# Written order for the transfers of one queue, late side stores, and four copies moved from VectorE to ScalarE, in a linear attention and mixture-of-experts kernel

## The chip, the core and the metric

The kernel runs on one core of a Trainium2 chip. A core has five engines with instruction streams of their own: TensorE (matrix products), VectorE, ScalarE (activation functions and copies), GpSimd (called POOL in the profile) and SyncE (SP), which here issues most of the DMA transfers. The metric is the device time of one execution in microseconds; less is better. Three timed executions of the kernel before gave 733.79 us in the median (732.57 to 734.19).

## What is computed

Two sublayers follow each other, each on normalized input and with its output normalized and added back. The first is a linear attention over 8 batches of 512 rows by 256 columns, the second a mixture of 8 experts of which each row uses two. `_layernorm` has no scale or shift.

```python
x = L0_attn_x                                   # (8, 512, 256)
x = x + _layernorm(_L0_attn_ref(_layernorm(x), Wq, bq, Wk, bk, Wv, bv, gamma))
x = x + _layernorm(_L0_ffn_ref(_layernorm(x), W1, b1, W2, b2, gate_W, shared_W, shared_b, gamma, beta))

# inside _L0_ffn_ref, flat has 4096 rows of 256
probs = softmax(flat @ gate_W)
topk_w, topk_idx = top_k(probs, 2)
combine = (one_hot(topk_idx, 8) * (topk_w / topk_w.sum(-1))[..., None]).sum(1)
out = 0.5 * gelu(flat @ shared_W + shared_b)
for e in range(8):
    h = gelu(flat @ W1[e] + b1[e])              # 256 -> 1024
    out = out + combine[:, e:e+1] * (h @ W2[e] + b2[e])
out = layernorm(out) * gamma + beta
```

All data are 32-bit floats.

## The kernel before

**Fronts.** `front(b)` computes, for one batch of 512 rows, the attention sublayer, the shared part of the second sublayer and the routing. It is a generator whose pieces are interleaved with those of other batches by `front_round`, after a table of starting rounds. On the way it stores three things in DRAM: the rows after the first sublayer (`x1_d`, line 542; the profile calls this tensor `x_d`), the shared part, which is where the sums of the second sublayer begin (`acc_d`, line 572), and the eight weights of each row (`comb_d`, line 620). GpSimd then scatters every row twice, once for each chosen expert, into slots of the DRAM tensor `xs` (line 669). A row in `xs` carries its 256 values, its eight weights and its number.

`comb_d`, `x1_d` and `shift_d` are also read by a dense pass at the end of the program (from line 1111), which computes rows by all experts. It runs only if the routing overflowed its slots, and it does not run with this data: `n_steps` is zero.

**Jobs.** A job is a stretch of 256 slots of one expert, or a tile of 128 slots. There are 37 jobs, numbered 0 to 36 here; the list is built at lines 685 to 694. Jobs 29 and 33 to 36 are tiles of 128 whose expert is known only at run time (`MORE = 5`). For each job:

- `fetch(k)` loads the slots, `xr` (line 705); it is called two jobs ahead, at the start of job k - 2.
- `turn(k)` transposes them on TensorE into two PSUM buffers and copies these to `rT`: the first half on VectorE, the second on ScalarE (`transposed`, lines 361 and 362). It is called before the last one or two row tiles of job k - 1.
- `routed(k)` computes the first layer in eight pieces on TensorE (`ph`, line 727, into a pool of four PSUM buffers), the activation on ScalarE (`h`, line 732), then the second layer (`po`, line 765) for every 128 rows. VectorE adds the bias and scales (`y`, lines 769 and 773), and GpSimd adds the rows into `acc_d` by an indirect DMA (line 776). Each such scatter waits for the scatters of the job before it. The last two jobs (`CLOSE = 2`) scatter nothing: their rows are added on TensorE, in `close`.

Weights are loaded by `load_w`: first-layer weights (line 207) go round three buffers, second-layer weights and biases (lines 210 and 212) round two. It is called when a job ends and the next one has another expert.

**Endings.** `back(b)` finishes a batch when all its scatters are in: it loads the sums (`accb`, line 831) and the rows of the first sublayer (`xb`, line 834), `finish_rows` normalizes twice on VectorE with square roots and the last addition on GpSimd (lines 801 to 823), and line 841 stores the output. A hand-written plan ties these steps to pieces of jobs: batches 0 to 4 lie under jobs 16 to 30, batches 5 to 7 under jobs 33 to 36. Batch 7 goes through `close` instead: at line 849 ScalarE adds a shift to `xb`; TensorE gathers in `fin` the sums (line 855) and the rows of the last two jobs (line 864); VectorE normalizes.

**What sets the order.** The streams of TensorE, VectorE and ScalarE keep the order in which the program writes them (the `manual_schedule` at line 969). GpSimd keeps the written order through `in_turn`, which chains each instruction behind the one before with `behind`, an ordering without a wait. SP's transfers had no such chain: a scheduler could put a transfer ahead of others that are written before it. One pair was chained by hand: the first `xr` load after the reading of the expert numbers, through `turns["SP"]`. In every stream an instruction that waits holds up all that stand behind it.

Of the kernel before, what the change touches and what calls it, by code (L numbers as in the profile page):

```python
# [16 lines left out]
def kernel(  # L17
# [21 lines left out]
    nc = tc.nc  # L39
# [54 lines left out]

    turns = {"on": False, "last": None, "dmas": []}

    def behind(ins, name):
        tc.add_manual_dep(  # L100
# [17 lines left out]
        return ins  # L118


    xs = dram.tile([SLOTS, DX], F32, name="xs")


# [11 lines left out]

    def load_x(b):
        t = act.tile([P, NT, D], F32, tag="x", name=f"x_{b}", bufs=XB)
        nc.sync.dma_start(t, x[b].rearrange("(p t) d -> p t d", t=NT))
# [7 lines left out]

    NK = 2 * ND
    wn = const.tile([P, NK, D + 1], F32, name="wn")
    nc.sync.dma_start(wn[:, 0:ND, 0:D], Wk.rearrange("(o p) i -> p o i", p=P))
    nc.sync.dma_start(wn[:, ND:NK, 0:D], Wq.rearrange("(o p) i -> p o i", p=P))  # L150
    rows = E * NH
    NR = rows + 3 * ND
    col_stage = act.tile([NR, P], F32, tag="h", name="col_in", bufs=10)
    nc.sync.dma_start(col_stage[0:rows, :], b1.rearrange("e (c p) -> (e c) p", p=P))
    for j, v in enumerate((bk, bq, bv)):
        r = rows + j * ND
        nc.sync.dma_start(col_stage[r : r + ND, :], v.rearrange("(c p) -> c p", p=P))
    load_x(1)

    NV = D + 2  # L160
    wvx = const.tile([P, ND, NV], F32, name="wvx")
    nc.sync.dma_start(wvx[:, :, 0:D], Wv.rearrange("(c p) i -> p c i", p=P))
    bqb = const.tile([P, D], F32, name="bqb")
    nc.sync.dma_start(bqb, bq.partition_broadcast(P))
    bkb = const.tile([P, D], F32, name="bkb")
    nc.sync.dma_start(bkb, bk.partition_broadcast(P))
    gam = const.tile([P, 1], F32, name="gam")
    nc.sync.dma_start(gam, attn_gamma.partition_broadcast(P))

    wsg = const.tile([P, ND, D + E], F32, name="wsg")  # L170
    nc.sync.dma_start(wsg[:, :, 0:D], shared_W.rearrange("(c p) d -> p c d", p=P))
    nc.sync.dma_start(wsg[:, :, D : D + E], gate_W.rearrange("(c p) e -> p c e", p=P))
    bsh = const.tile([P, D], F32, name="bsh")
    nc.sync.dma_start(bsh, shared_b.partition_broadcast(P))
    load_x(2)

    for b in range(3, XB):
# [2 lines left out]

    pad = const.tile([P, CT, DX], F32, name="pad")
    nc.vector.memset(pad, 0.0)
    nc.sync.dma_start(acc_d[B * C :, :].rearrange("(p t) d -> p t d", p=P), pad[:, :, 0:D])
    nc.gpsimd.iota(
        pad[:, :, DX - 1].bitcast(I32), pattern=[[1, CT]], base=B * C, channel_multiplier=CT
    )
    for e in range(E):
        nc.sync.dma_start(
            xs[e * CAP : (e + 1) * CAP, :].rearrange("(j p t) d -> p j (t d)", p=P, t=CT),
            pad.rearrange("p t d -> p (t d)").unsqueeze(1).to_broadcast([P, CAP // CS, CT * DX]),  # L190
        )
    nc.sync.dma_start(
        xs[E * CAP :, :].rearrange("(j p) d -> p j d", p=P),
        pad[:, 0, :].unsqueeze(1).to_broadcast([P, MORE, DX]),
    )
# [2 lines left out]
    def load_w(e, which=(1, 2), name=""):  # L198

        v = ids[e - E] if e >= E else e  # L200

        def of(w):
            return w[bass.ds(v, 1)] if e >= E else w[v : v + 1]

        if 1 in which:
            w1[e] = act.tile([P, ND, H], F32, tag="w1", name=f"w1_{name}{e}", bufs=NW1)
            nc.sync.dma_start(w1[e], of(W1).rearrange("o (c p) h -> p (o c) h", p=P))
        if 2 in which:
            w2[e] = act.tile([P, NH, D], F32, tag="w2", name=f"w2_{name}{e}", bufs=NW2)
            nc.sync.dma_start(w2[e], of(W2).rearrange("o (c p) d -> p (o c) d", p=P))  # L210
            b2b[e] = act.tile([P, D], F32, tag="b2", name=f"b2_{name}{e}", bufs=NW2)
            nc.sync.dma_start(b2b[e], of(b2).rearrange("o d -> (o d)").partition_broadcast(P))
# [4 lines left out]
    nc.sync.dma_start(fgam, ffn_gamma.partition_broadcast(P))  # L217
    fbet = const.tile([P, D], F32, name="fbet")
    nc.sync.dma_start(fbet, ffn_beta.partition_broadcast(P))

# [135 lines left out]
            pts.append(pt[:, 0 : src.shape[1] * P])  # L356
        return pts

    def transposed(dst, src, name):
        pts = transposes(src, name)  # L360
        nc.vector.tensor_copy(dst[:, 0, :], pts[0])  # L361
        nc.scalar.copy(dst[:, 1, :], pts[1])

    def mid(name):
        return act.tile([P, ND, NV], F32, tag="mid", name=name, bufs=10)

    scatters, fills = [], {}

    shifts = const.tile([P, B, NT], F32, name="shifts")

# [1 line left out]
    def front(b):  # L372
# [169 lines left out]
        nc.sync.dma_start(rows_of(x1_d, b), xt)  # L542
        if b + XB < B:
            load_x(b + XB)
        stats = ln_stats([xt[:, t, :] for t in range(NT)], f"c{b}")
# [23 lines left out]
            )  # L569
        yield "A"  # L570
        nc.scalar.activation(acc, acc, AF.Gelu)
        st = nc.sync.dma_start(rows_of(acc_d, b), acc)
        unordered(st, "acc")
        fills[b] = st.ins

# [40 lines left out]
        ))  # L616
        in_turn(nc.gpsimd.tensor_tensor(row[:, :, D : D + E], wb, both, ALU.add))
        in_turn(nc.gpsimd.tensor_copy(row[:, :, DX - 1].bitcast(I32), token[:, b, :]))

        nc.sync.dma_start(rows_of(comb_d, b), row[:, :, D : D + E])  # L620


        shape3 = [P, NT, E]
# [73 lines left out]
    def fetch(k):  # L697
        if k >= len(jobs):
            return
        e, s0, s1 = jobs[k]  # L700
        nt = (s1 - s0) // P
        assert s0 < FIRST or not fronts
        xrs[k] = act.tile([P, CT, DX], F32, tag="xr", name=f"xr_{k}", bufs=4)[:, 0:nt, :]
        r0 = e * CAP + s0 if e < E else E * CAP + (e - E) * P
        ld = nc.sync.dma_start(xrs[k], xs[r0 : r0 + s1 - s0, :].rearrange("(p t) d -> p t d", t=nt))
        if "SP" in turns:
            behind(ld, turns.pop("SP"))
        unordered(ld, "scatter", [ins for b, ins in scatters if s0 >= FIRST or b <= EARLY])

    def turn(k):  # L710
        if k >= len(jobs):
            return
        e, s0, s1 = jobs[k]
        rTs[k] = act.tile([P, ND, CS], F32, tag="rT", name=f"rT_{k}", bufs=2)[:, :, 0 : s1 - s0]
        transposed(rTs[k], xrs[k][:, :, 0:D], f"r{k}")

    def routed(k):
        e, s0, s1 = jobs[k]
# [109 lines left out]
    def back(b):  # L828
        acc = act.tile([P, NT, D], F32, tag="acc", name=f"accb_{b}", bufs=4)
        last = max(n for (e, s1), n in ends.items() if s1 <= room(b, e))  # L830
        ld = nc.sync.dma_start(acc, rows_of(acc_d, b))
        unordered(ld, "acc", [fills[b], *adds[last - 1]])
        xt = act.tile([P, NT, D], F32, tag="x", name=f"xb_{b}", bufs=XB)
        nc.sync.dma_start(xt, rows_of(x1_d, b))
        yield
        if b < B - 1:
            yield from finish_rows(
                [acc[:, t, :] for t in range(NT)], [xt[:, t, :] for t in range(NT)],
                shifts[:, b, :], f"{b}", True,
            )  # L840
            nc.sync.dma_start(out[b].rearrange("(p t) d -> p t d", t=NT), xt)
        else:
            yield from close(acc, xt)


    def close(acc, xt):
# [47 lines left out]
        for h, (mv, rs) in enumerate(parts):  # L894
            for m, t in enumerate(halves[h]):
                nc.vector.tensor_scalar(
                    acc[:, t, :], acc[:, t, :], mv[:, m, 0:1], rs[:, m : m + 1],
                    ALU.subtract, ALU.mult,
                )
            t0, t1 = halves[h][0], halves[h][-1] + 1  # L900
            nc.vector.tensor_tensor(xt[:, t0:t1, :], xt[:, t0:t1, :], acc[:, t0:t1, :], ALU.add)
            nc.sync.dma_start(
                out[b].rearrange("(p t) d -> p t d", t=NT)[:, t0:t1, :], xt[:, t0:t1, :]
            )

# [11 lines left out]
    def check_room():  # L917
        G = len(groups)
        pcnt = bank("p_cnt")[:, 0, 0 : (G + 2) * E].rearrange("p (s e) -> p s e", e=E)
        for s, b in enumerate([*groups, EARLY, B - 1]):  # L920
# [20 lines left out]
        nc.sync.dma_start(  # L941
            shift_d.rearrange("(b p t) o -> p b (t o)", b=B, p=P), shifts
        )
        shape = [P, MORE, E]
# [263 lines left out]
```

## Time and profile before

The profiled execution took 734.14 us, of which 732.4 us lie between its first and its last instruction (the span). Times in the profile count from the start of the span.

| engine | busy, us | share of the span | instructions |
|---|---|---|---|
| TensorE, products | 677.7 | 93% | 3359 |
| VectorE | 285.0 | 39% | 1096 |
| ScalarE | 233.1 | 32% | 540 |
| GpSimd | 294.1 | 40% | 419 |

The page cuts the span into 40 slices. From 165 us to 696 us TensorE's busy share is 9 (90% or more) in every slice but one, at 220 to 238 us. It is lower in several slices of the fronts and in the last two. The DMA engines moved 142.24 MB, 194 GB/s over the span.

| transfer | count | KB each | median us from issue to landing |
|---|---|---|---|
| `w`, either layer's weights | 70 | 1024 | 6.2 |
| `b`, bias of the second layer | 35 | 128 | 6.5 |
| `xr`, 256 slots | 32 | 265 | 2.9 |
| `xr`, 128 slots | 5 | 132.5 | 2.1 |
| `accb` | 8 | 512 | 4.7 |
| `xb` | 8 | 512 | 4.1 |
| `comb_d` store | 8 | 16 | 2.8 |
| scatter into `acc_d` | 67 | | 5.2 |

How to read the lines shown further on. A line of a timeline has the start and the length in us, the engine, the line of the program, the operation, what is written and read, the shape and the count; in brackets the engine's idle time before it and what ended that. A line of the view of waits has who waited for whom, then the total in us, the number of times and the longest. A line of the view of stretches has the stretch, its length, the busy time of TensorE's products, of its weight loads, of VectorE, ScalarE and GpSimd, then the granted clock of TensorE (1.00 is full), the busy share of the DMA engines and GB/s. SPq is SP's queue, which issues transfers; `x1`, `x2` are counts. The chain of waits goes back from the last instruction, at each step to what released it.

### The profile page before, as it was taken

To read this page: it belongs to the slowest core of one execution; us is meant where nothing else is said; L and a number is where in the kernel's file an instruction comes from. 1 tells how busy PE (TensorE), PEld (TensorE's weight loads), DVE (VectorE), ACT (ScalarE), POOL (GpSimd) and SP (SyncE) were. 2 spreads that over 40 slices of the span, in tenths; PEclk is the share of its full clock that TensorE was granted. 3 is DMA by queue.
4 is the path that set the end of the run, shared out by engine and by line. 5 is a ranking of instruction groups with operands and counts; after the bars stand their busy time and mean duration, and the time that the engine had idled before them with its cause. 6 is when DMAs were issued, how large, how long until landed. Compare 5 with 4: busy or idle time off the path is not lost.

```text
span 732.4 us, 10181 instructions
## 1 busy us (share of the span) xinstructions
PE 677.7 (93%) x3359; PEld 591.3 (81%) x3359; DVE 285.0 (39%) x1096; ACT 233.1 (32%) x540; POOL 294.1 (40%) x419
## 2 busy tenths in 40 slices
PE   6998997939998999999999999999999999999981
PEld 4887786727887888888888888888888888988860
DVE  3658868854545143111111112314132132511555
ACT  4444534314331423223223322322332232322430
POOL 3304318775564625122122113433625235442392
PEclk9999999978998999999999999999999999999996
DMA  7994123443377868667667667556686886977841
GB/s 236 381 354 156 72 74 145 148 160 136 112 216 197 252 184 225 200 187 217 174 205 191 190 201 210 156 129 186 205 234 182 259 257 166 287 221 202 267 134 60
DMA packets 88855, 142.24 MB, mean 194 GB/s; under 512 B 11158, under 2 KB 63324, under 8 KB 88796
## 3 DMA queue, kind: packets, MB, share of 16 engines
q1 hardware_dynamic: 76076, 124.05, 52.2%
q0 software_dynamic: 12720, 17.47, 12.1%
q8 instruction: 29, 0.48, 0.3%
q14 instruction: 30, 0.25, 0.1%
HBM read 101.68 MB, written 39.82 MB: 193 GB/s over the span
## 4 chain that ended last, share of the span: by engine, by line
PE 82%; DVE 10%; POOL 2%; DMA 2%; issue 2%; ACT 1%; SPq 0%; POOLq 0%; DVEq 0%
PE ph L727 32%; PE po L765 31%; PE pg L402 3%; PE psh L561 3%; PE py L526 2%; PE pa L482 2%; PE pt_r L353 2%; PE pq L468 1%; PE pt_x L353 1%; DVE x L539 1%; PE puq L424 1%; PE puk L424 1%; DVE junk L440 1%; DVE st_c L332 1%; DMA acc_d<-y,xr 1%
## 5 line engine op out<-in xcount | busy, mean ns | idle before, releaser
L727 PE MATMUL ph<-rT,w 128*128 128x256 f32 (+1 forms) x1184 | 248.7, 368 | 3.6 <-DVE rT L361 3.6
L765 PE MATMUL po<-w,h 128*128 128x256 f32 x1104 | 244.7, 379 | 0.0
L727 PEld LDWEIGHTS ph<-rT,w 128*128 128x128 f32 x1184 | 214.7, 192 | 31.6 <-DVE rT L361 4.4
L765 PEld LDWEIGHTS po<-w,h 128*128 128x128 f32 x1104 | 207.0, 190 | 26.5
L776 POOL DMA_INDIRECT acc_d<-y,xr x67 | 105.4, 1573 | 291.6 <-DVE y L773 268.8
L732 ACT ACTIVATE h<-ph,cols 128x256 f32<-128x256 f32 x256 | 120.9, 473 | 310.8 <-PE ph L727 310.6
L769 DVE TENSOR_TENSOR y<-po,b 128x256 f32<-128x256 f32 x69 | 29.2, 424 | 180.3 <-PE po L765 180.3
L361 DVE COPY rT<-pt_r 128x256 f32<-128x256 f32 (+1 forms) x37 | 15.0, 404 | 170.4 <-PE pt_r L353 166.8
L669 POOL DMA_INDIRECT xs<-xn,slot x64 | 64.7, 1011 | 21.2 <-issue 17.5
L526 PE MATMUL py<-wm,xT 128*128 128x256 f32 x128 | 29.2, 380 | 3.8 <-DVE wm L517 3.8
L561 PE MATMUL psh<-wsg,xfT 128*128 128x264 f32 x128 | 30.0, 388 | 1.5 <-DVE xfT L361 1.5
L526 PEld LDWEIGHTS py<-wm,xT 128*128 128x128 f32 x128 | 23.7, 189 | 7.9 <-DVE wm L517 3.7
L561 PEld LDWEIGHTS psh<-wsg,xfT 128*128 128x128 f32 x128 | 24.1, 191 | 5.7 <-DVE xfT L361 1.9
L482 PE MATMUL pa<-wk,g 128*128 128x258 f32 x64 | 17.2, 415 | 9.9 <-DVE acc L566 9.9
L732 ACT ACTIVATE h<-ph,b1m 128x128 f32<-128x128 f32 x40 | 14.6, 367 | 30.2 <-PE ph L727 27.0
L402 PE MATMUL pg<-xn 128*128 128x128 f32 (+1 forms) x128 | 23.9, 341 | 0.0
L773 DVE TENSOR_SCALAR y<-y,xr 128x256 f32<-128x256 f32 x64 | 22.7, 355 | 2.3
L353 PE MATMUL pt_r<-identd,xr 128*128 128x128 f32 x138 | 21.5, 274 | 1.8 <-DMA xr<-xs 1.2
L482 PEld LDWEIGHTS pa<-wk,g 128*128 128x128 f32 x64 | 13.0, 207 | 12.4 <-DVE acc L566 10.3
L402 PEld LDWEIGHTS pg<-xn 128*128 128x128 f32 x128 | 21.1, 201 | 2.3 <-DVE xn L530 0.2
L445 POOL TENSOR_TENSOR inv<-sq,mhalf 128x4 f32<-128x4 f32 x8 | 8.5, 1059 | 32.5 <-DVE sq L440 32.4
L353 PEld LDWEIGHTS pt_r<-identd,xr 128*128 128x128 f32 x138 | 17.2, 143 | 5.2 <-ACT h L732 1.4
(195 smaller groups left out, 645.7 us busy)
## 6 DMA issues: line engine op xcount, KB each, us to landing
w<-in_L_ffn_W_dram SPq DMA_DIRECT2D x70, 1024.0 KB, 6.2
xs<-pad SPq DMA_DIRECT2D x8, 1060.0 KB, 15.2
xr<-xs SPq DMA_DIRECT2D x32, 265.0 KB, 2.9
b<-in_L_ffn_b_dram SPq DMA_DIRECT2D x35, 128.0 KB, 6.5
x<-in_L_attn_x_dram SPq DMA_DIRECT2D x8, 512.0 KB, 6.6
x_d<-x SPq DMA_DIRECT2D x8, 512.0 KB, 2.9
acc_d<-acc SPq DMA_DIRECT2D x8, 512.0 KB, 4.5
xb<-x_d SPq DMA_DIRECT2D x8, 512.0 KB, 4.1
```

The costliest lines, as they stand in the source:

```text
L353: nc.tensor.transpose(pt[:, t * P : (t + 1) * P], src[:, t, i * P : (i + 1) * P], ident)
L402: nc.tensor.matmul(pg[:, c, c * P : D], xn[:, t, c * P : (c + 1) * P], xn[:, t, c * P : D], start=(t == 0), stop=(t == NT - 1),)
L482: nc.tensor.matmul(pa[:, c, 0:NV], g[:, i, c * P : (c + 1) * P], wk[:, i, :], start=(i == 0), stop=(i == ND - 1),)
L526: nc.tensor.matmul(py[:, t, :], xT[:, i, tt * P : (tt + 1) * P], wm[:, i, 0:D], start=(i == 0), stop=(i == ND - 1),)
L561: nc.tensor.matmul(ps[:, t, 0 : D + E], xT[:, i, tt * P : (tt + 1) * P], wsg[:, i, :], start=(i == 0), stop=(i == ND - 1),)
L669: ins = in_turn(nc.gpsimd.indirect_dma_start(out=xs[:, :], out_offset=bass.IndirectOffsetOnAxis(ap=slot[:, t, j : j + 1], axis=0), in_=row ...
L727: nc.tensor.matmul(ph, w1[e][:, i, c * P : (c + 1) * P], rT[:, i, :], start=(i == 0), stop=(i == ND - 1),)
L732: nc.scalar.activation(ht, ph, AF.Gelu, bias=(cols[:, e * NH + c : e * NH + c + 1] if e < E else b1m[:, e - E, c : c + 1]))
L765: nc.tensor.matmul(po, hs[c][:, t * P : (t + 1) * P], w2[e][:, c, :], start=(c == 0), stop=(c == NH - 1),)
L769: nc.vector.tensor_tensor(y[:, t, :], po, b2b[e], ALU.add)
L773: nc.vector.tensor_scalar_mul(y[:, t, :], y[:, t, :], xrs[k][:, t, D + e : D + e + 1] if e < E else one_w)
L776: ins = in_turn(nc.gpsimd.indirect_dma_start(out=acc_d[:, :], out_offset=bass.IndirectOffsetOnAxis(ap=xrs[k][:, t, DX - 1 : DX].bitcast(I3 ...
```

## The change

Three edits:

1. `transposed` gets a switch `on_scalar`. With it, ScalarE makes both copies, the first ahead of the second. `turn(k)` sets it for `k > 37 - 5`, that is for jobs 33 to 36.
2. The stores to `comb_d` are no longer issued inside `front`. Each is put in a list; `keep_combs` issues what is in the list, once when the front of batch 7 begins and once after the last front.
3. All transfers of SP go through a new function `move`, which chains each behind the transfer written before it once `turns["on"]` is set. Loads of registers on SP (the number of dense steps and the expert numbers) are put in the same chain.

```diff
+    def move(dst, src):
+        ins = nc.sync.dma_start(dst, src)
+        if turns["on"]:
+            next_move(ins)
+        return ins
+
+    def next_move(ins):
+        if turns["move"]:
+            behind(ins, turns["move"])
+        turns["move"] = ins.ins.name
...
-    def transposed(dst, src, name):
+    def transposed(dst, src, name, on_scalar=False):
         pts = transposes(src, name)
-        nc.vector.tensor_copy(dst[:, 0, :], pts[0])
+        if on_scalar:
+            nc.scalar.copy(dst[:, 0, :], pts[0])
+        else:
+            nc.vector.tensor_copy(dst[:, 0, :], pts[0])
         nc.scalar.copy(dst[:, 1, :], pts[1])
...
-        nc.sync.dma_start(rows_of(comb_d, b), row[:, :, D : D + E])
+        combs.append((b, row))
...
-        ld = nc.sync.dma_start(xrs[k], xs[r0 : r0 + s1 - s0, :].rearrange("(p t) d -> p t d", t=nt))
-        if "SP" in turns:
-            behind(ld, turns.pop("SP"))
+        ld = move(xrs[k], xs[r0 : r0 + s1 - s0, :].rearrange("(p t) d -> p t d", t=nt))
...
-        transposed(rTs[k], xrs[k][:, :, 0:D], f"r{k}")
+        transposed(rTs[k], xrs[k][:, :, 0:D], f"r{k}", k > len(jobs) - MORE)
...
-        ld = nc.sync.dma_start(acc, rows_of(acc_d, b))
+        ld = move(acc, rows_of(acc_d, b))
         unordered(ld, "acc", [fills[b], *adds[last - 1]])
         xt = act.tile([P, NT, D], F32, tag="x", name=f"xb_{b}", bufs=XB)
-        nc.sync.dma_start(xt, rows_of(x1_d, b))
+        move(xt, rows_of(x1_d, b))
...
+    def keep_combs():
+        for b, row in combs:
+            move(rows_of(comb_d, b), row[:, :, D : D + E])
+        combs.clear()
+
     def front_round():
         nonlocal rnd
         if rnd in starts:
             b = starts[rnd]
+            if b >= XN:
+                keep_combs()
...
         if rnd > max(starts) and not fronts:
+            keep_combs()
             check_room()
...
             for ins in loads:
                 if ins.ins.engine == mybir.EngineType.Pool:
                     in_turn(ins)
+                if ins.ins.engine == mybir.EngineType.SP:
+                    next_move(ins)
...
-            turns["SP"] = loads[-1].ins.name
+            for ins in loads:
+                next_move(ins)
```

Every other `nc.sync.dma_start` outside the dense pass becomes `move` with the same arguments, those in `load_w` too.

More of the change, by code (lines that the diff above doesn't have):

```diff
@@ L93, in after @@
             )
-    turns = {"on": False, "last": None, "dmas": []}
+    turns = {"on": False, "last": None, "dmas": [], "move": None}
     def behind(ins, name):
@@ L137, in load_x @@
         t = act.tile([P, NT, D], F32, tag="x", name=f"x_{b}", bufs=XB)
-        nc.sync.dma_start(t, x[b].rearrange("(p t) d -> p t d", t=NT))
+        move(t, x[b].rearrange("(p t) d -> p t d", t=NT))
         x_tiles[b] = t
@@ L148 @@
     wn = const.tile([P, NK, D + 1], F32, name="wn")
-    nc.sync.dma_start(wn[:, 0:ND, 0:D], Wk.rearrange("(o p) i -> p o i", p=P))
-    nc.sync.dma_start(wn[:, ND:NK, 0:D], Wq.rearrange("(o p) i -> p o i", p=P))
+    move(wn[:, 0:ND, 0:D], Wk.rearrange("(o p) i -> p o i", p=P))
+    move(wn[:, ND:NK, 0:D], Wq.rearrange("(o p) i -> p o i", p=P))
     rows = E * NH
@@ L153 @@
     col_stage = act.tile([NR, P], F32, tag="h", name="col_in", bufs=10)
-    nc.sync.dma_start(col_stage[0:rows, :], b1.rearrange("e (c p) -> (e c) p", p=P))
+    move(col_stage[0:rows, :], b1.rearrange("e (c p) -> (e c) p", p=P))
     for j, v in enumerate((bk, bq, bv)):
         r = rows + j * ND
-        nc.sync.dma_start(col_stage[r : r + ND, :], v.rearrange("(c p) -> c p", p=P))
+        move(col_stage[r : r + ND, :], v.rearrange("(c p) -> c p", p=P))
     load_x(1)
@@ L161 @@
     wvx = const.tile([P, ND, NV], F32, name="wvx")
-    nc.sync.dma_start(wvx[:, :, 0:D], Wv.rearrange("(c p) i -> p c i", p=P))
+    move(wvx[:, :, 0:D], Wv.rearrange("(c p) i -> p c i", p=P))
     bqb = const.tile([P, D], F32, name="bqb")
-    nc.sync.dma_start(bqb, bq.partition_broadcast(P))
+    move(bqb, bq.partition_broadcast(P))
     bkb = const.tile([P, D], F32, name="bkb")
-    nc.sync.dma_start(bkb, bk.partition_broadcast(P))
+    move(bkb, bk.partition_broadcast(P))
     gam = const.tile([P, 1], F32, name="gam")
-    nc.sync.dma_start(gam, attn_gamma.partition_broadcast(P))
+    move(gam, attn_gamma.partition_broadcast(P))
     wsg = const.tile([P, ND, D + E], F32, name="wsg")
-    nc.sync.dma_start(wsg[:, :, 0:D], shared_W.rearrange("(c p) d -> p c d", p=P))
-    nc.sync.dma_start(wsg[:, :, D : D + E], gate_W.rearrange("(c p) e -> p c e", p=P))
+    move(wsg[:, :, 0:D], shared_W.rearrange("(c p) d -> p c d", p=P))
+    move(wsg[:, :, D : D + E], gate_W.rearrange("(c p) e -> p c e", p=P))
     bsh = const.tile([P, D], F32, name="bsh")
-    nc.sync.dma_start(bsh, shared_b.partition_broadcast(P))
+    move(bsh, shared_b.partition_broadcast(P))
     load_x(2)
@@ L182 @@
     nc.vector.memset(pad, 0.0)
-    nc.sync.dma_start(acc_d[B * C :, :].rearrange("(p t) d -> p t d", p=P), pad[:, :, 0:D])
+    move(acc_d[B * C :, :].rearrange("(p t) d -> p t d", p=P), pad[:, :, 0:D])
     nc.gpsimd.iota(
@@ L187 @@
     for e in range(E):
-        nc.sync.dma_start(
+        move(
             xs[e * CAP : (e + 1) * CAP, :].rearrange("(j p t) d -> p j (t d)", p=P, t=CT),
@@ L191 @@
         )
-    nc.sync.dma_start(
+    move(
         xs[E * CAP :, :].rearrange("(j p) d -> p j d", p=P),
@@ L206, in load_w @@
             w1[e] = act.tile([P, ND, H], F32, tag="w1", name=f"w1_{name}{e}", bufs=NW1)
-            nc.sync.dma_start(w1[e], of(W1).rearrange("o (c p) h -> p (o c) h", p=P))
+            move(w1[e], of(W1).rearrange("o (c p) h -> p (o c) h", p=P))
         if 2 in which:
             w2[e] = act.tile([P, NH, D], F32, tag="w2", name=f"w2_{name}{e}", bufs=NW2)
-            nc.sync.dma_start(w2[e], of(W2).rearrange("o (c p) d -> p (o c) d", p=P))
+            move(w2[e], of(W2).rearrange("o (c p) d -> p (o c) d", p=P))
             b2b[e] = act.tile([P, D], F32, tag="b2", name=f"b2_{name}{e}", bufs=NW2)
-            nc.sync.dma_start(b2b[e], of(b2).rearrange("o d -> (o d)").partition_broadcast(P))
+            move(b2b[e], of(b2).rearrange("o d -> (o d)").partition_broadcast(P))
     for e in range(NW1):
@@ L216 @@
     fgam = const.tile([P, D], F32, name="fgam")
-    nc.sync.dma_start(fgam, ffn_gamma.partition_broadcast(P))
+    move(fgam, ffn_gamma.partition_broadcast(P))
     fbet = const.tile([P, D], F32, name="fbet")
-    nc.sync.dma_start(fbet, ffn_beta.partition_broadcast(P))
+    move(fbet, ffn_beta.partition_broadcast(P))
     identd = const.tile([P, ND, D], F32, name="identd")
@@ L365, in mid @@
         return act.tile([P, ND, NV], F32, tag="mid", name=name, bufs=10)
-    scatters, fills = [], {}
+    scatters, fills, combs = [], {}, []
     shifts = const.tile([P, B, NT], F32, name="shifts")
@@ L541, in front @@
             )
-        nc.sync.dma_start(rows_of(x1_d, b), xt)
+        move(rows_of(x1_d, b), xt)
         if b + XB < B:
@@ L571, in front @@
         nc.scalar.activation(acc, acc, AF.Gelu)
-        st = nc.sync.dma_start(rows_of(acc_d, b), acc)
+        st = move(rows_of(acc_d, b), acc)
         unordered(st, "acc")
@@ L840, in back @@
             )
-            nc.sync.dma_start(out[b].rearrange("(p t) d -> p t d", t=NT), xt)
+            move(out[b].rearrange("(p t) d -> p t d", t=NT), xt)
         else:
@@ L901, in close @@
             nc.vector.tensor_tensor(xt[:, t0:t1, :], xt[:, t0:t1, :], acc[:, t0:t1, :], ALU.add)
-            nc.sync.dma_start(
+            move(
                 out[b].rearrange("(p t) d -> p t d", t=NT)[:, t0:t1, :], xt[:, t0:t1, :]
@@ L939, in check_room @@
         nc.vector.tensor_copy(steps_i, steps_f)
-        nc.sync.dma_start(
+        move(
             shift_d.rearrange("(b p t) o -> p b (t o)", b=B, p=P), shifts
```

## Prediction

> **What bounds it now.** I read the chain of waits first: TensorE holds 82% of it, so only time in which TensorE stands still can go or come.
>
> ```profile
> PE 82%; DVE 10%; POOL 2%; DMA 2%; issue 2%; ACT 1%; SPq 0%; POOLq 0%; DVEq 0%
> ```
>
> Then TensorE's own waits. Between 12 and 690 us not one of them names a transfer. Two rows belong to the change: the turned rows `rT` came late from VectorE twice, and the gathered rows `xr` came late from a transfer once.
>
> ```profile
> PE ph L727 <- DVE rT L361: 3.6, 2, 2.0
> ...
> PE pt_r L353 <- DMA xr<-xs: 1.2, 1, 1.2
> ```
>
> TensorE's timeline puts all three in the last 45 us. I number the jobs from 0, so the last four are 33 to 36.
>
> ```profile
> 689.71 1.67 PE L765 MATMUL po<-w,h 128*128 128x256 f32 x7
> 692.98 3.84 PE L727 MATMUL ph<-rT,w 128*128 128x128 f32 x32 [1.60 <-DVE rT L361]
> 698.05 0.41 PE L353 MATMUL pt_r<-identd,xr 128*128 128x128 f32 x2 [1.23 <-DMA xr<-xs]
> 698.30 3.62 PE L765 MATMUL po<-w,h 128*128 128x256 f32 x16
> 703.95 3.84 PE L727 MATMUL ph<-rT,w 128*128 128x128 f32 x32 [2.03 <-DVE rT L361]
> ...
> 711.07 3.62 PE L765 MATMUL po<-w,h 128*128 128x256 f32 x16
> ```
>
> Line 2 is job 35, lines 3 and 4 the turning for job 36 and job 35's second half, line 5 job 36. VectorE has `finish_rows` of batch 5 and 6 queued ahead of its copy, so ScalarE's half of job 35's `rT`, ready at 688.3, waits for VectorE's at 692.9. Now SP's queue in the same stretch:
>
> ```profile
> 683.71 0.82 SPq L831 DMA_DIRECT2D accb<-acc_d  x2
> 684.76 0.39 SPq L207 DMA_DIRECT2D w<-in_L_ffn_W_dram  x1
> 685.39 0.39 SPq L210 DMA_DIRECT2D w<-in_L_ffn_W_dram  x1
> 686.01 2.78 SPq L212 DMA_DIRECT2D b<-in_L_ffn_b_dram  x1
> 688.84 1.85 SPq L705 DMA_DIRECT2D xr<-xs  x1
> ...
> 701.52 0.33 SPq L831 DMA_DIRECT2D accb<-acc_d  x1
> ```
>
> Two loads of sums, two weights of 1 MB, a bias and job 36's `xr` leave at once. The bias took 2.78 us to issue and `xr` 1.85, where such issues take 0.3 to 0.5 elsewhere: the queue is full. The stretches of 2 us (last columns: clock, share of the DMA engines, GB/s) agree:
>
> ```profile
> 686.00:688.00 2.00, 2.00 (x20) 1.98 (x19) 0.60 (x2) 1.66 (x5) 0.81 (x1) 1.00 0.92 360
> ...
> 692.00:694.00 2.00, 1.02 (x9) 1.02 (x10) 1.93 (x9) 0.27 (x1) 0.00 (x0) 1.00 1.10 343
> 694.00:696.00 2.00, 2.00 (x21) 2.00 (x20) 2.00 (x10) 1.57 (x5) 1.46 (x1) 1.00 1.03 357
> 696.00:698.00 2.00, 0.82 (x8) 0.63 (x6) 2.00 (x10) 0.98 (x3) 1.77 (x4) 1.00 1.03 358
> ```
>
> From 686 to 698 the DMA engines are full, at 334 GB/s on the mean of the six stretches. Landings come in order of issue: the second-layer weight 11.5 us after its issue (696.9), the bias at 697.5, `xr` 9.1 us after (697.95). What is put ahead of them delays them.
>
> **The copies.** Four VectorE copies of 128x128 (0.28 us each) become four ScalarE copies (0.26 each). For jobs 33 and 34 TensorE did not wait: no change. ScalarE stands idle 5.40 us before job 35's activations, so the copies cost nothing there. Job 35's `rT` is complete at about 688.6, TensorE is free at 691.38, and its first layer runs 691.4 to 695.2: 1.60 us earlier. This gain is given back at once, since the next instruction turns job 36's `xr`, which lands at 697.95 whatever the copies do. Job 36's `rT` is then whole at about 699.0 instead of 703.9, well before TensorE is free at 701.92: 2.03 us go. By the copies alone the gain is 2.03 us.
>
> **The order of SP's queue.** In SP's stream of the changed kernel as built, each load `xb` now stands behind its `accb`. Before, the scheduler had put all eight far ahead; those of batches 5 and 7 left at 482.70 and 568.45.
>
> (a) Batches 5 and 6: two `xb` of 524 KB now go between the `accb` pair and the two weights. 1.05 MB at 334 GB/s is 3.1 us, so job 36's `xr` lands at 701.05. [...] From below the bound is 0 (they find room), from above 3.5 us (301 GB/s, the mean of 684 to 700). With 3.1, TensorE is idle from 695.2 to 701.05, runs job 35's second layer from 701.3 to 704.9, and starts job 36 at 704.9: 0.95 us later than before, in place of 2.03 earlier.
>
> (b) Batch 7: `xb` follows `accb` of batch 7, which waits for job 34's scatter. ScalarE reads it in `close` at line 849, and line 849 stands ahead of job 36's eight activations:
>
> ```profile
> 698.50 0.27 ACT L362 COPY rT<-pt_r 128x128 f32<-128x128 f32 x1 [1.21 <-PE pt_r L353]
> 698.66 1.70 ACT L849 ACTIVATE xb<-xb,shifts 128x256 f32<-128x256 f32 x4
> 704.70 3.55 ACT L732 ACTIVATE h<-ph,b1m 128x128 f32<-128x128 f32 x8 [4.34 <-PE ph L727]
> ```
>
> Now the row at 698.66 waits for a load that cannot leave before 701.95 (701.52 plus the 0.43 between two issues). The scatter left at 694.54 and took 7.0 us; job 33's, under full engines throughout, took 8.5. As the engines stay full about 3 us longer, I take 7.7: `accb` leaves at 702.2, `xb` at 702.65. Loads of `xb` landed in 2.4 to 5.3 us, median 3.2, and of `accb` in 3.4 to 6.0, median 4.7; standing behind an `accb`, 4.7 is nearest: 707.3. Then line 849, 1.7 us (709.0), the first activation, 0.45 (709.5). `ph` has four buffers, so TensorE has done four of eight pieces and needs one freed: four more at 0.46 (3.7 over 8) end at 711.3. `fin` takes 1.72 and 1.73: 714.8. There the last second layer starts, 711.23 in the chain before: **3.6 us later**. Ends of (b): landing after 2.4 from 701.95 gives +0.7, after 6.0 from 703.45 gives +5.6.
>
> **The clock.** Job 35's gap grows to 5.8 us. Stretches earlier in this trace:
>
> ```profile
> 154.50:164.30 9.80, 0.00 (x0) 0.00 (x0) 3.86 (x14) 0.17 (x3) 7.93 (x13) 0.61 0.55 171
> 164.30:170.50 6.20, 6.16 (x19) 5.19 (x20) 2.24 (x8) 1.30 (x4) 4.77 (x8) 0.51 0.48 173
> ...
> 233.30:238.60 5.30, 5.30 (x14) 4.22 (x14) 3.92 (x18) 0.95 (x2) 2.13 (x6) 0.50 0.65 183
> ```
>
> After 9.9 us of rest the clock was 0.51, and it was 0.50 after a pause of only 3.6 us with four small products in it (229.7 to 233.3); there 32 `ph` products took 9.66 us instead of 6.91. [...] I add nothing; the upper end holds the 2.75.
>
> **Moves that cost nothing.** The eight `comb_d` stores (0.55 us each on SP) move behind `acc_d` of batch 2 and to the end of the fronts. TensorE's wait of 9.89 us at 164 stems from VectorE waiting for GpSimd's `rs_b` (7.5 us), and GpSimd's order is the same. First-layer weights for jobs 3 and 4 leave after x1 stores, 197.4 to 203 and 218.8 to 239, against first use at 251 and 270 and a median landing of 6.2. The `xr` of jobs 33 to 35 leave after the weights; the tightest, job 35's, goes from 670.0 to 678 and is needed at 687.5. `accb` of batch 4 now waits for batch 3's store (622.05), leaves at 622.45, lands at 627.1, and VectorE starts on it 2.9 us later; its copy for job 30 then ends at 633.7, TensorE wants it at 634.2: nothing, or 0.8 us with a landing of 6.0. SP's register load moves from 727.6 (0.30 us) to the middle; SP waits until 729.6 for the last store either way.
>
> **Sum.** +3.6 us on a span of 732.4, which is 736.0; the execution of 734.14 us becomes 737.7. That execution is 0.35 above the median of 733.79, so the median goes to **737.4**.
>
> **Rivals.** *ScalarE's wait alone*: the two `xb` of (a) find room, but batch 7's does not come in time. With a landing of 3.9 us (between the two medians) from 701.95 it is there at 705.8, and the same steps give +2.1: 735.9. For it: the scatter's landing alone sets it; against: full engines. *Faster*: (a) costs nothing, job 34's scatter leaves 0.3 us sooner (no copy ahead of its product on VectorE) and lands in 5.2 us, the median of all such scatters: 699.4. `xb` leaves at 699.9, lands in 2.4 at 702.3, and the last second layer starts at 709.7: -1.5, 732.3. The turning point is `xb` landing at 703.8. Against it: neither scatter after 684 took less than 7.0. *The clock on top*: low clock reaches into job 36 and `fin`: 2.75 more, 740.2. *Cancelled*: gain and losses meet within 0.2% (1.5 us, what a measurement of this kernel can tell from no change). That the order is not as written is excluded by SP's built stream.
>
> **Chances.** Forecast 0.50, ScalarE alone 0.20, clock on top 0.14, cancelled 0.08, faster 0.08 (a gain from a stage that I count as unchanged is in it). So faster 0.08, within 0.2% 0.08, slower 0.84. Range: from +0.7 (734.5) to 740.2.
>
> **What would show it.** Right: `xb` issues at 684 to 686 ahead of the weights; a TensorE wait of 5 to 6 us for `xr`; line 849 starting only at 706 to 708 behind a transfer; job 36's activations after it; stages before 680 as before. Wrong: line 849 still near 699, `xr` landing near 698, or a loss before 680 us.

## The result, and the profile after

| kernel | median of the runs, us | runs | ratio to before (95%) |
|---|---|---|---|
| before | 733.79 (732.57 to 734.62) | 5 | |
| changed | 737.82 (736.44 to 740.97) | 5 | 1.007 (1.0049 to 1.0092) |

The medians differ by 4.0 us. The ratio in the table is not their quotient (1.0055): at 1.007 the change costs 5.1 us, and its interval reaches from 3.6 to 6.8. The profiled execution of the changed kernel took 740.07 us with a span of 738.3, so it lies 2.2 us above the median of its runs. Where its trace is used for sizes, this has to be kept in mind.

The first view is TensorE's own waits from 620 us to the end (who waited for what, in all, times, longest). The lines of the program have moved by 9 to 13: 727 is now 740, 765 is 778, 849 is 862, and every transfer has the line of `move`, 122.

```profile
PE pt_r L365 <- DMA xr<-xs: 6.0, 1, 6.0
PE ph L740 <- ACT h L745: 2.1, 1, 2.1
PE ph L740 <- DVE rT L376: 0.7, 1, 0.7
```

The two waits for VectorE's `rT` in the tail, 1.60 and 2.03 us, are gone. The wait for `xr` has grown from 1.2 to 6.0 us, and a wait for ScalarE's `h` is new. The third line is job 30's small slip at 633 us, which the prediction had named as possible. TensorE's timeline of the tail:

```profile
690.82 3.73 PE L740 MATMUL ph<-rT,w 128*128 128x128 f32 x32
700.59 0.66 PE L365 MATMUL pt_r<-identd,xr 128*128 128x128 f32 x2 [6.03 <-DMA xr<-xs]
701.04 5.15 PE L778 MATMUL po<-w,h 128*128 128x256 f32 x16
706.02 1.95 PE L740 MATMUL ph<-rT,w 128*128 128x128 f32 x16
710.03 2.97 PE L740 MATMUL ph<-rT,w 128*128 128x128 f32 x16 [2.06 <-ACT h L745]
712.80 2.67 PE L868 MATMUL fin<-accb,identd 128*128 128x512 f32 x4
...
717.03 3.62 PE L778 MATMUL po<-w,h 128*128 128x256 f32 x16
```

Line 1 is job 35's first layer, then come job 36's turning, job 35's second layer and job 36's first layer, cut in two by the wait for ScalarE. The last line started at 711.07 before: it is 5.96 us later, and the profiled execution is 5.93 us longer. Everything that the change costs this execution is therefore in front of that line. Before 680 us nothing is lost: job 33 starts at 676.33, against 676.73.

ScalarE's timeline shows what held `h`:

```profile
708.02 1.71 ACT L862 ACTIVATE xb<-xb,shifts 128x256 f32<-128x256 f32 x4 [6.47 <-DMA xb<-x_d]
709.63 1.58 ACT L745 ACTIVATE h<-ph,b1m 128x128 f32<-128x128 f32 x5
```

The addition to batch 7's `xb`, at 698.66 before, starts at 708.02 behind a transfer, and job 36's activations stand behind it. SP's queue shows why the two transfers are late:

```profile
683.79 0.33 SPq L122 DMA_DIRECT2D accb<-acc_d  x1
684.17 0.42 SPq L122 DMA_DIRECT2D xb<-x_d  x1
684.65 0.42 SPq L122 DMA_DIRECT2D accb<-acc_d  x1
685.11 0.43 SPq L122 DMA_DIRECT2D xb<-x_d  x1
686.13 0.80 SPq L122 DMA_DIRECT2D w<-in_L_ffn_W_dram  x2
687.16 3.22 SPq L122 DMA_DIRECT2D b<-in_L_ffn_b_dram  x1
690.42 2.33 SPq L122 DMA_DIRECT2D xr<-xs  x1
...
703.23 0.33 SPq L122 DMA_DIRECT2D accb<-acc_d  x1
703.60 0.43 SPq L122 DMA_DIRECT2D xb<-x_d  x1
```

Two `xb` stand ahead of the weights and of `xr`, and batch 7's `xb` is the last load of all. Finally three stretches of 4 us; the last three columns are the granted clock, the share of the DMA engines and GB/s:

```profile
696.00:700.00 4.00, 0.00 (x0) 0.00 (x0) 2.60 (x11) 0.00 (x0) 3.52 (x8) 0.66 0.87 294
700.00:704.00 4.00, 3.42 (x9) 2.84 (x10) 3.59 (x8) 0.48 (x2) 3.83 (x6) 0.50 0.75 215
...
712.00:716.00 4.00, 4.00 (x13) 2.47 (x13) 0.00 (x0) 0.73 (x2) 3.75 (x7) 0.70 0.03 6
```

Before, the clock was 1.00 in all three. Here TensorE runs at half of it after the gap, and again for a while after the wait for ScalarE: the second half of job 36's first layer and the first part of `fin` take 2.97 and 2.67 us instead of some 1.9 each.

### The profile page after: what moved, and what is told of

Its sections match the earlier page's. It is cut to its first block, busy times and chain, and to the rows that moved or that the text cites. A ratio compares the mean times of both kernels' runs of the same rounds, so it can differ in the third digit from the quotient of the medians.

```text
span 738.3 us, 10158 instructions
## 1 busy us (share of the span) xinstructions
PE 682.0 (92%) x3359; PEld 594.1 (80%) x3359; DVE 284.6 (39%) x1092; ACT 233.7 (32%) x544; POOL 295.1 (40%) x419
## 5 line engine op out<-in xcount | busy, mean ns | idle before, releaser
L576 PE MATMUL psh<-wsg,xfT 128*128 128x264 f32 x128 | 32.7, 413 | 1.5 <-DVE xfT L376 1.5
L576 PEld LDWEIGHTS psh<-wsg,xfT 128*128 128x128 f32 x128 | 26.0, 206 | 6.6 <-DVE xfT L376 1.9
L497 PE MATMUL pa<-wk,g 128*128 128x258 f32 x64 | 16.9, 411 | 9.3 <-DVE acc L581 9.3
L836 POOL TENSOR_TENSOR xb<-xb,accb 128x256 f32<-128x256 f32 x28 | 20.4, 728 | 2.3
```

Source lines behind the costliest of these rows:

```text
L497: nc.tensor.matmul(pa[:, c, 0:NV], g[:, i, c * P : (c + 1) * P], wk[:, i, :], start=(i == 0), stop=(i == ND - 1),)
L576: nc.tensor.matmul(ps[:, t, 0 : D + E], xT[:, i, tt * P : (tt + 1) * P], wsg[:, i, :], start=(i == 0), stop=(i == ND - 1),)
```

## The experiments

Each kernel ran beside the kernel before on the same chip, in four groups, whose medians of before were 732.94, 733.15, 733.65 and 733.53 us. Compare by the difference or the ratio, not by the absolute time.

The last column is from the one trace of each kernel: the time from the issue of the first `accb` of the pair (683.71 us before) to the start of the last second layer (711.07 before). Executions reach this pair at different times, from 681.89 to 684.57 us, so absolute times in two tails do not compare; this column does. Where the pair itself was moved, it has no entry.

| kernel | median, us | against before, us | ratio (95%) | tail, us |
|---|---|---|---|---|
| before | | | | 27.36 |
| changed | 737.82 | +4.0 | 1.007 (1.0049 to 1.0092) | 33.24 |
| copies alone | 731.64 | -1.3 | 0.998 (0.9967 to 0.9992) | 26.75 |
| order and stores, no copies | 737.55 | +4.6 | 1.0072 (1.0051 to 1.0093) | 32.74 |
| changed, all three `xb` early | 732.54 | -0.4 | 0.9996 (0.9978 to 1.0013) | 26.63 |
| changed, `comb_d` stores in place | 736.31 | +3.4 | 1.0049 (1.003 to 1.0069) | 31.47 |
| changed, `xb` 7 early: (a) alone | 735.25 | +2.1 | 1.003 (1.0018 to 1.0042) | 29.70 |
| changed, `xb` 5 and 6 early: (b) alone | 736.05 | +2.9 | 1.0047 (1.0033 to 1.0062) | 30.53 |
| (a) alone, gap filled | 733.25 | +0.1 | 1.0 (0.9988 to 1.0012) | 26.92 |
| all `xb` early, job 36's `xr` early | 732.41 | -0.7 | 0.9989 (0.9978 to 1.0) | |
| and job 35's `w2` first | 733.97 | +0.3 | 1.0002 (0.9987 to 1.0017) | |
| and `fin` last | 731.67 | -2.0 | 0.9974 (0.9964 to 0.9983) | |
| copies alone, gap filled | 730.45 | -3.2 | 0.9959 (0.9948 to 0.9971) | 24.90 |
| changed, gap filled | 739.82 | +6.3 | 1.0093 (1.0071 to 1.0115) | 32.84 |

Against before, the tails differ by what the medians differ by, within 0.9 us, except for the changed kernel, whose trace was one of a long execution (5.9 us against 4.0). So what these edits cost or gain arises in the tail.

### Which of the three edits

The copies alone are the kernel before with the first edit:

```diff
-        transposed(rTs[k], xrs[k][:, :, 0:D], f"r{k}")
+        transposed(rTs[k], xrs[k][:, :, 0:D], f"r{k}", k > len(jobs) - MORE)
```

> The kernel before with the first edit alone: ScalarE makes both copies for jobs 33 to 36, SP's queue as before. My theory (the loss comes from the loads put into the last 50 us): the 1.60 us wait of job 35 goes but is taken back by the landing of job 36's rows at about 698, and the 2.03 us wait of job 36 goes, so 2.0 us less than before, 731.8; a fall of the clock in job 35's gap of 2.8 us could take back up to 1.5. Rival (two copies in a row on ScalarE hold up its activations and are part of the loss): no faster than before, 733.8 or more.

The next is the changed kernel with this line taken back.

> The changed kernel without the first edit: VectorE makes the first copy again, the written order and the late stores stay. My theory: job 36's rows land at 700 to 701 and batch 7's rows hold up ScalarE until 707 to 708 whatever the copies do, so the time is that of the changed kernel, 736.5 to 739. Rival (the copies on ScalarE are the loss): back to 733.8.

The copies are a gain by themselves, and the new order costs about the same with the copies (1.007) or without (1.0072). Beside the new order no gain of theirs shows: job 36 then waits for transfers, not for its `rT`.

Third, the changed kernel with the `comb_d` stores issued inside the front again.

```diff
-        combs.append((b, row))
+        move(rows_of(comb_d, b), row[:, :, D : D + E])
```

> The changed kernel with the eight comb_d stores issued again inside the fronts, in written order. My theory: they cost nothing in either place, 737.8 within 1. Rival (the stores in place hold up SP for GpSimd's order and so later loads): 739 or more; if the late stores were a loss: 736.5 or less.

The time is 1.5 us below the changed kernel's, but the two intervals overlap, so this does not settle whether the late stores cost something. The traces give no sign of it: the first `accb` of the pair left at 684.57 us here and between 681.97 and 683.79 in seven kernels with the late stores, so up to there those lose nothing.

### Which of the `xb`

In these three kernels chosen `xb` are loaded when job 31 begins, and all else stays as changed: those of batches 5, 6 and 7 in the first, that of 7 in the second, those of 5 and 6 in the third.

```diff
+    early = {}
+    def load_xb(b):
+        xt = act.tile([P, NT, D], F32, tag="x", name=f"xb_{b}", bufs=XB)
+        move(xt, rows_of(x1_d, b))
+        return xt
...
-        xt = act.tile([P, NT, D], F32, tag="x", name=f"xb_{b}", bufs=XB)
-        move(xt, rows_of(x1_d, b))
+        xt = early[b] if b in early else load_xb(b)
...
+            if (k, n) == (31, 0):
+                for b in (5, 6, 7):
+                    early[b] = load_xb(b)
```

> The changed kernel with the three loads xb of batches 5, 6 and 7 written at job 31, some 35 us ahead of the last sums, everything else in written order. My theory: both delays (the rows of job 36 behind 1 MB more, ScalarE waiting for batch 7) go, the gain of the copies is left: 731.8, as with the copies alone, 733 if the clock falls in a gap of some 3 us. Rival (the written order or the late stores cost something elsewhere, in the fronts or the middle): 735 or more.

> The changed kernel with only batch 7's xb written at job 31; the xb of batches 5 and 6 stay among the last sums and weights. This leaves the first delay alone: two loads of 524 KB less one that is gone stand ahead of job 36's rows. My theory: rows land at about 700.6, TensorE stands still some 6 us and comes back at half clock, ScalarE no longer waits: 0.95 us by the delay and 1.7 by the clock, 735 to 736.5. Rival (ScalarE's wait for batch 7 is all of the loss): at or below the time before, 733.8 or less.

> The changed kernel with the xb of batches 5 and 6 written at job 31 and batch 7's left behind its sums. This leaves the second delay alone. My theory: job 36's rows land near 698 as before, but line 862 on ScalarE starts only when batch 7's rows are in, at about 705.5 to 706, and job 36's activations behind it: about 2 us above before, 735.5 to 737. Rival (the queue being 1 MB fuller is all of the loss): 732 or less.

With all three early the loss is gone, so it lies in the place of these three loads. But no gain over before can be told either (0.9996, where the copies alone gave 0.998; the intervals overlap, so a small cost of the chain of `move` or of the late stores is not excluded).

(a) alone costs 2.1 us. TensorE waited 5.94 us for `xr` in it. ScalarE took batch 7's `xb` at 700.74 without a wait, so nothing of (b) is left. (b) alone costs 2.9 us; its ScalarE timeline has the wait of the changed kernel:

```profile
705.65 1.71 ACT L868 ACTIVATE xb<-xb,shifts 128x256 f32<-128x256 f32 x4 [7.30 <-DMA xb<-x_d]
```

Both kernels have the gain of the copies in them, so the measure for either is the kernel with all `xb` early (-0.4 us): (a) takes 2.5 us from it, (b) 3.3, both together 4.4. Job 36 cannot pass its first four pieces before ScalarE is back, so a part of what (a) takes should lie in the time that (b) takes anyway. The times alone do not show this overlap: by the ratios it is 2.5 and 3.7 against 5.4 us, within the intervals. The tails agree with it: 3.1 and 3.9 us alone, and 4.8 to 6.6 in the four traces with both.

### The clock

(a) alone again, with twelve products of constants put into job 35's `po` before job 36's turning. They change no result, since the first own product starts the buffer anew.

```diff
+            if k == len(jobs) - 2:
+                po = pair(f"po_{k}_{t}")[:, 0, 0:D]
+                for _ in range(12):
+                    nc.tensor.matmul(po, ident, identd[:, 0, :], start=True, stop=True)
             if t == max(nt - 2, 0):
                 turn(k + 1)
-            po = pair(f"po_{k}_{t}")[:, 0, 0:D]
+            if k != len(jobs) - 2:
+                po = pair(f"po_{k}_{t}")[:, 0, 0:D]
```

> The kernel of e4 with twelve products of constants put on TensorE in the gap between job 35's first layer and the turning of job 36's rows; their result is written over by the next product. They take about 5.2 of the 6 us of the gap. My theory of the clock: it stays at 1.00, job 35's second layer takes 3.5 us instead of about 5.1, and the time falls by 1.5 to 2 against e4. Rival (the long second layer comes from late weights or from contention, not from the clock): the time of e4, or more.

TensorE's timeline of (a) alone, around the gap:

```profile
699.88 0.66 PE L365 MATMUL pt_r<-identd,xr 128*128 128x128 f32 x2 [5.94 <-DMA xr<-xs]
700.33 5.64 PE L778 MATMUL po<-w,h 128*128 128x256 f32 x16
```

And that of the kernel with the gap filled:

```profile
694.18 5.34 PE L777 MATMUL po<-identd 128*128 128x256 f32 x24
699.72 0.41 PE L365 MATMUL pt_r<-identd,xr 128*128 128x128 f32 x2 [0.19 <-DMA xr<-xs]
699.96 3.62 PE L783 MATMUL po<-w,h 128*128 128x256 f32 x16
```

`xr` lands at the same time. The second layer takes 3.62 instead of 5.64 us, and the time falls by 2.0. So against before the whole loss of (a) alone is the clock: the later landing itself is paid for by the copies.

The same was tried on the copies alone, with eight such products of 128x256 in the gap.

> The copies alone (731.64 us, ratio 0.998, where the step 'The copies' of the prediction had 2.03 us) with eight products of 128x256 more, of constants, written into job 35's po before its own products, whose first one overwrites them. They fill the gap of 3.8 us before job 36's xr. Theory (the missing 0.7 us and more are the clock: job 35's second layer took 5.30 us after that gap, against 3.62 at full clock): the second layer takes 3.6 us again and the time is 1.2 to 1.7 us below the copies alone, 729.9 to 730.4. Rival (the copies gain less for another reason, the slow products being hidden by what follows them): 731.4 to 731.9.

TensorE's timeline of the copies alone:

```profile
697.65 0.41 PE L353 MATMUL pt_r<-identd,xr 128*128 128x128 f32 x2 [3.79 <-DMA xr<-xs]
697.89 5.30 PE L768 MATMUL po<-w,h 128*128 128x256 f32 x16
...
710.05 3.62 PE L768 MATMUL po<-w,h 128*128 128x256 f32 x16
```

And with the gap filled:

```profile
692.26 3.62 PE L767 MATMUL po<-identd 128*128 128x256 f32 x16
696.07 0.41 PE L353 MATMUL pt_r<-identd,xr 128*128 128x128 f32 x2 [0.19 <-DMA xr<-xs]
696.32 3.62 PE L773 MATMUL po<-w,h 128*128 128x256 f32 x16
...
706.79 3.62 PE L773 MATMUL po<-w,h 128*128 128x256 f32 x16
```

From the turning to the last second layer it is 12.40 us in the first (710.05 less 697.65) and 10.72 in the second: 1.68 us less, all of it in job 35's second layer. (That `xr` also landed 1.6 us earlier in this one execution is not the filler's doing: the whole tail came earlier, its first `accb` at 681.89 us against 683.30.) The medians fell by 1.9 against their own runs of before. At 0.9959 this kernel has the lowest median of all, and it is faster than before and than the changed kernel.

Between this kernel and (a) alone with its gap filled (0.9959 and 1.0), in both of which the clock is kept up (job 35's second layer takes 3.62 us), lie 3.0 us. That is what the later landing of `xr` costs by itself; the prediction's steps make it 2.98 (2.03 us earlier against 0.95 later).

Last, the changed kernel itself with twelve such products in its gap.

> The changed kernel (737.82 us) with twelve products of constants (128x256) more, written into job 35's po before job 36's turning; the first own product overwrites them. They fill most of the gap of 6.0 us before job 36's xr, so that the clock stays at 1.00 behind it. The prediction gave the clock no place in its sum, since job 36 cannot pass the first half of its first layer until ScalarE has come back from its wait for batch 7's xb. By that step: job 35's second layer takes 3.6 us in place of 5.15, TensorE only waits longer for ScalarE (3.5 to 4 us in place of 2.06), and the time is 737.2 to 738 us, as the changed kernel's. Rival (the clock adds on top, as it did for part (a) alone, where the same filler took 2.0 us off): 735.6 to 736.6 us. Between them: the wait for ScalarE holds, but the second half of job 36 and fin run at full clock, 736.6 to 737.2.

Its TensorE timeline:

```profile
700.04 3.62 PE L783 MATMUL po<-w,h 128*128 128x256 f32 x16
703.50 1.95 PE L740 MATMUL ph<-rT,w 128*128 128x128 f32 x16
709.35 3.63 PE L740 MATMUL ph<-rT,w 128*128 128x128 f32 x16 [3.91 <-ACT h L745]
...
716.27 3.62 PE L783 MATMUL po<-w,h 128*128 128x256 f32 x16
```

The second layer is back at 3.62 us, and nothing is gained by it: TensorE only waits longer for ScalarE, 3.91 in place of 2.06. The clock is lost after that wait instead (16 products of `ph` in 3.63 us, where 1.95 is usual, at a granted clock of 0.66 from 708 to 712 us). The median is 2.0 us above the changed kernel's and above the 737.2 to 738 that was expected; the intervals overlap, so a loss against the changed kernel is not shown, but the rival's 735.6 to 736.6 is excluded.

### What comes after the late `xr`

With all `xb` early, job 36's `xr` was also loaded one job earlier, when job 33 starts, into the second half of job 33's own buffer.

```diff
-        xrs[k] = act.tile([P, CT, DX], F32, tag="xr", name=f"xr_{k}", bufs=4)[:, 0:nt, :]
+        if k == len(jobs) - 1:
+            xrs[k] = whole[k - 3][:, 1:2, :]
...
-        fetch(k + 2)
+        if k < len(jobs) - 3:
+            fetch(k + 2)
+        if k == len(jobs) - 4:
+            fetch(k + 3)
```

> The kernel of e3 with job 36's rows fetched one job earlier, ahead of the sums of batch 5, into the unused half of job 33's buffer. My theory: the gap before the turning of job 36 goes, what is next is the landing of job 35's second-layer weight (696.9 before) and of batch 7's sums (about 706): 1 to 2.5 us below e3, 729.5 to 731. Rival (the end is set by batch 7's sums alone): as e3.

It missed. The gap did not go, it changed its owner, as TensorE's timeline of this kernel shows:

```profile
699.25 5.38 PE L787 MATMUL po<-w,h 128*128 128x256 f32 x16 [3.94 <-DMA w<-in_L_ffn_W_dram]
```

So `xr` had hidden that job 35's second-layer weight lands only at about 699 in that kernel. In the next kernel this weight and its bias go ahead of job 36's first-layer weight and of batch 6's `accb`; for the latter, batch 6's first step in the plan moves one piece later.

```diff
-            for n, w in ((NW1, 1), (NW2, 2)):
+            for n, w in ((NW1, 1), (NW2, 2)) if k != len(jobs) - 4 else ((NW2, 2), (NW1, 1)):
```

> As the run with the earliest xr (all three xb early, job 36's xr loaded at the start of job 33; 732.41 us, its bound a wait of 3.94 us for job 35's second-layer weight), and in the fetches at the start of job 34 the second-layer weight and bias of job 35 now go ahead of the first-layer weight of job 36 and of batch 6's sums. Theory 1 (the queue hands its transfers out in order, so the weight lands as much earlier as 1 to 1.5 MB at about 334 GB/s take, 3 to 4.5 us): the wait before job 35's second layer goes, and TensorE is next held for batch 7's sums, in fin: 729.5 to 731.5 us. Rival (the end is set by the landing of job 34's scatter and batch 7's accb behind it, whatever comes before): the idle time only moves from job 35 to fin, with no gain beyond 0.5 us: 732 to 732.8 us.

Again a miss, and again a wait moved on. TensorE's timeline:

```profile
705.97 3.75 PE L883 MATMUL fin<-accb,identd 128*128 128x512 f32 x4 [3.29 <-DMA accb<-acc_d]
709.52 2.97 PE L892 MATMUL fin<-y,pick 128*128 128x256 f32 x8
```

Batch 7's sums hold `fin`, and after the gap of 3.29 us `fin` runs at half clock (3.75 and 2.97 us, against 1.88 and 1.89 in the kernels where nothing was idle before it; granted clock 0.61 from 704 to 708 us and 0.54 from 708 to 712). The rival had it right: idle time moved from job 35 to `fin`. The last of this row moves batch 7's last step one piece later in the plan (10 becomes 11), which puts `fin` behind job 36's second layer.

> The run before with batch 7's fin products written after job 36's first layer and as late as its plan allows (one piece later), so that batch 7's sums have the time of job 36's products to land. If batch 7's sums are the last thing that TensorE waits for (theory 1): their wait of some 3 us goes and the time is 727.5 to 730 us, under both kernels and under the copies alone (731.64). Rival (the closing stage on VectorE needs the sums in fin before the last second layer, and fin written late only moves its 3.4 us behind it): no gain, or up to 1.5 us slower than the run before.

TensorE now runs from 683 to 705 us without a gap of a microsecond, and the time is 2.3 us lower than the kernel before it in this row, 2.0 below before. Neither expectation was met in full (731.67 where 727.5 to 730 was forecast). VectorE's timeline shows the next bound:

```profile
717.28 0.88 DVE L918 SCALAR_TENSOR_TENSOR accb<-accb,rs_dz,fbet 128x256 f32<-128x256 f32 x2 [3.04 <-POOL rs_dz L335]
```

The closing stage waits for GpSimd, which is busy with the last additions of `finish_rows` until 716.23. This kernel cannot be told from the copies alone (0.9974 and 0.998), nor quite from the copies with the gap filled (0.9959): the intervals overlap. A GpSimd relieved of these additions was not tried.

## Why the prediction was right

The forecast of 737.4 us stands against a median of 737.82, and the mechanism is the one that it gave: `xb` left at 684 to 685 us ahead of the weights, TensorE waited 6.03 us for `xr`, line 849 (now 862) started at 708.02 behind a transfer, and job 36's activations stood behind it. That the number fits so closely is in part luck, as the step (b) shows. By its own steps:

- *The copies*: the mechanism is shown, the size is off. The 1.60 us of job 35 are given back to `xr` as said, and in the changed kernel both waits for `rT` are gone. But the copies alone gave 1.3 us (0.6 to 2.4 by the interval), not 2.03. The missing term is the clock: by the step's own numbers a gap of 2.8 us is left before `xr` (3.79 in the trace), and it did not ask what that does to the products behind it. It costs 1.68 us by the traces with and without the filler. With the gap filled the copies gave 3.2 us (2.1 to 3.8), and the tail is 2.5 us shorter than before.
- *(a)*: shown. From the issue of the first `accb` of the pair to the turning for job 36 it is 14.3 us before (683.71 to 698.05) and 16.8 in the changed kernel (683.79 to 700.59): 2.5 us for the two `xb`, where 3.1 was worked out from 334 GB/s, the mean from 686 to 698 us. Over the traces it is 14.2 to 14.9 us in five without these two `xb` there and 16.2 to 16.9 in six with them, 2.2 on the mean. So that rate made the delay too long, by 0.6 to 0.9 us. For (a) without (b) the step gives +0.95 us, or +0.35 with 2.5. Measured: +2.1, and +0.1 once the clock is kept up.
- *(b)*: shown, and the step that sets the time. Batch 7's `xb` was said to leave at 702.65 and to land at 707.3; it left at 703.60, as job 34's scatter took 8.6 us and not 7.7, and ScalarE took it at 708.02, 4.4 us later and not 4.7. The last second layer, 714.8 in the sum, started at 717.03. These 2.2 us are 0.5 from the later start of job 36's second half, and 0.9 and 0.8 from the half clock in that half and in `fin`. This last term was not in the sum; it stood only in the rival with the clock on top. In the kernel without copies the last second layer started at 714.71, but that is no confirmation: its tail began 1.8 us earlier (first `accb` at 681.97), and it lost clock after ScalarE's wait too. Where this clock was kept (`comb_d` stores in place), the tail is 4.1 us longer than before; where it was lost, 5.4 to 5.9. The sum had 3.6.
- *The clock*: half clock came after the gap (0.50 from 700 to 704 us; 5.15 us for job 35's second layer, 1.5 more than 3.62). The 2.75 at the upper end of the forecast is 9.66 less 6.91 us, the extra time of the 32 products at 233 us in the trace before; the forecast itself added nothing. That the clock adds little there, because job 36 waits for ScalarE anyway, is borne out by the filler that gained nothing. The prediction looked at one gap only, though: the wait for ScalarE costs clock too.
- *Moves that cost nothing*: nothing before 680 us contradicts it except the 0.7 us of job 30, foreseen as a possibility and made good by 676 us. The `comb_d` stores stay open, as told.
- *The rivals*: ScalarE alone forecast +2.1 us; (b) alone measured +2.9 (1.0033 to 1.0062, so at least 2.4), and in the changed kernel (a) is there too. Faster and cancelled fall. The clock on top (740.2) is what the profiled execution (740.07) looks like: the low clock did reach into job 36 and `fin` there, for 1.7 us, though it came from the wait for ScalarE and not from the gap that the rival named. The median lies at the forecast. By the ratio the forecast (1.0049) stands at the lower end of the interval and this rival (1.0087) inside it, so the rival is not shut out.

A slip in the ends of (b): by its own steps they are +0.6 and +5.7 us, not +0.7 and +5.6. Nothing rests on it.

What stays open is how many executions of the changed kernel lose clock after the wait for ScalarE, and with it how much of this is in the median. Three of the four traces that have both delays did.

## What to carry to other kernels

When a load is put in its written place, ask two things: what now stands behind it in the queue, and whose stream waits for it; a load that was far ahead for no reason of its own may have kept two engines out of each other's way. A gain that only makes an engine arrive earlier at a wait can be eaten by the clock (1.68 us in the copies alone); cheap products in the gap kept it up here, and added to the copies they were worth more (1.9 us) than the copies alone (1.3). But fill a gap only where no later wait takes its place: the same filler was worth 2 us with one wait behind it removed, and nothing with it in place. And measure two traces from a common event in front of the change, not from the start of the span.

## What the runs showed of the hardware

In these runs every gap of TensorE in the last 50 us from 3.29 us up was followed by slow products: 3.29, 3.49, 3.54, 3.79, 3.91, 3.94, 4.24, 5.94, 6.03 and 6.59 us, ten of ten. Job 35's second layer took 5.15 to 6.37 us after such a gap, against 3.62. By these runs the gap of 5.8 us that the prediction gave job 35 is one of that kind, and so is the copies' gap (3.79 us).

Shorter waits are not safe either, and the traces show a part of what it depends on. In the traces of before and of the changed kernel, from 100 us on and before the idle end, the clock falls to half seven times: at 156.72 and 231.82 us before, at 113.63, 158.00, 233.09, 697.31 and 710.96 us in the changed kernel. Each time it stays there for 3.41 us or two, three or four times that (3.41 to 13.65 us), and within a trace all of these begin on one raster of 3.41 us, that is, whole multiples of 3.41 us apart. So the lines here are cut along that raster; what the first busy time leaves of a stretch is TensorE's idle time in it. The changed kernel around its wait of 2.06 us for ScalarE:

```profile
707.54:710.96 3.42, 1.36 (x12) 1.17 (x12) 1.52 (x10) 2.84 (x9) 2.20 (x6) 1.00 0.34 140
710.96:714.37 3.41, 3.41 (x13) 2.51 (x12) 0.00 (x0) 1.35 (x4) 3.16 (x6) 0.50 0.00 0
```

The kernel before around its wait of 2.03 us for `rT`:

```profile
699.44:702.86 3.42, 2.48 (x12) 1.84 (x10) 2.79 (x7) 0.92 (x3) 3.25 (x5) 1.00 0.30 66
702.86:706.27 3.41, 2.32 (x20) 2.32 (x21) 3.37 (x13) 1.27 (x4) 3.24 (x5) 1.00 0.36 129
706.27:709.68 3.41, 3.41 (x20) 2.43 (x19) 0.81 (x4) 1.66 (x5) 2.81 (x8) 1.00 0.38 156
```

The first wait lay within one stretch, which was idle for 2.06 us, and the next stretch has the clock at 0.50. The second lay across two, idle for 0.94 and 1.09 us, and the clock stayed. Over both traces a stretch at full clock with 2.06 us or more of idle was followed by half clock in six of six cases, and so was one with 1.62 us; one with 1.42 us or less never was. In none of the seven was the stretch before the fall idle throughout (2.76 us of 3.41 at most). In the kernel without copies, a wait of 2.05 us was followed by `fin` in 3.20 us instead of 1.88 (granted clock 0.65 from 708 to 712 us); waits for ScalarE of 1.67 us in (b) alone and of 1.25 us with the `comb_d` stores in place left `fin` at 1.88. So a wait of about 2 us cost clock or not in these traces, and the two above differ in where they fall on the raster, while every one of 3.29 us or more in the last 50 us cost it. No run moved a wait along the raster on purpose.
